# One head of the first searched place copied out by ScalarE in the sums of an attention and expert block

## The chip, the core and the metric

The kernel runs on one core of a Trainium2 chip. TensorE does matrix products into PSUM, VectorE does elementwise work and reductions, ScalarE does activations and copies, GpSimd (POOL) elementwise work and indirect DMAs, and SyncE (SP) issues most plain DMAs. The metric is the device time of one execution in microseconds (us). The time before is 2557.42 us, the median of three runs.

## What is computed

One transformer block on x of 4 x 2048 x 256, modulated by c: a layer norm, causal attention with 8 heads of width 32 and a geometric bias, a gated residual, a second layer norm, and an expert layer (2 shared experts, the best 4 of 16 routed ones for each token) with its gated residual. Cut to what matters here:

```python
scores = jnp.einsum('bhqd,bhkd->bhqk', q, k) * scale
scores = jnp.where(causal[None, None], scores, -jnp.inf)
scores = scores + head_scales[None, :, None, None] * geo
attn = jax.nn.softmax(scores, axis=-1)
out = jnp.einsum('bhqk,bhkd->bqhd', attn, v).reshape(B, T, C)
x = x + ga * (out @ w_out)
...
x = x + gb * ffn(h)          # 2 shared experts, top 4 of 16 routed
```

The softmax subtracts each row's maximum, so the kernel computes the scores twice: once to find the maximum (the search), and once, transposed, for the exponentials and the sums.

## The kernel before

**Tiles.** The 8192 tokens are 16 blocks `i` of 512 (QB); four blocks make one sequence, and `qb = i % 4` is the place in it. The 8 heads are two groups `g` of four. The scale and the geometric bias are folded into the key weights, so a score is a plain product.

**The search of block i** (`max_steps`, `scores(t, ch)` at line 425). For 128 queries `t` and a chunk `ch` of up to 512 keys (`w` of them), four products, one for each head, run at once in four strips of 32 rows of TensorE. Two heads go to one place (`both`, named ps) and two to the next. VectorE then finds each head's maximum in each place with one TENSOR_REDUCE over both heads, and writes it to `parts`. Where the chunk holds the diagonal (`ch == qb`), it first adds the causal mask to the last 128 columns of both heads, with `c_pair`, the mask repeated twice. `split` joins the parts, and `turn` brings the maxima into the layout that the sums need (`mT`).

**The sums of block i** (`sum_steps`, line 660 on). For each 128 keys `kb`, `probabilities` makes four transposed scores in two places (st): four products of 32 rows, four of 3 rows that subtract the maxima (the profile's st<-mT,unit), on the diagonal a mask product. Two exps on ScalarE write them to `pt` (p), one for each place. `weigh(kb, 0)` is the product with v (av) and `weigh(kb, 1)` the product with ones (dv). VectorE forms the reciprocal of dv at the end of each group (rd).

**PSUM.** `mring` (line 149) has three places of two banks, 128x2x512 f32; each of the two heads of a place has a bank. A place is taken in program order by the next user and is free when all that read it are done. A set of scores takes two places, an st takes two. `accp` has the other two banks, for av and dv during the sums.

**Order.** Every engine runs its instructions in the order in which the program issues them (`Pinned`). A block alternates between two phases. `fill_in` mixes projections, the expert work and searches of block i+1. Then come the sums of block i, with `state["summing"]` true; the searches of block i+1 that are left (`rest`) are placed among them. In the sums, step n issues: st of kb n; av of kb n-1; then, where there is one, a set of scores; dv of kb n-1; then small steps (norms, the choice of experts) and the `tick` that issues gathers and scatters. `paced` (line 496) makes each of these indirect DMAs wait for the last ScalarE instruction issued so far.

**Rings in SBUF.** `small` has three buffers for each tag, among them `log`, the router's logits, written by `logits` in `turn_steps` (line 846) between two sums and read by `choice_steps` in the sums that follow. `probs` has two buffers for each tag and is there once the setup is done.

Of the kernel before, what the change touches and what calls it, by code (L numbers as in the profile page):

```python
# [12 lines left out]
F32 = mybir.dt.float32  # L13
AF = mybir.ActivationFunctionType
ALU = mybir.AluOpType
AX = mybir.AxisListType
# [3 lines left out]
P = 128  # L20
QB = 512
TT = QB // P
# [70 lines left out]
def adaln_block_kernel(  # L93
# [13 lines left out]
    nc = Engines(tc)  # L107
# [5 lines left out]
    R = router.shape[2]  # L113
# [30 lines left out]
    small = ctx.enter_context(tc.tile_pool(name="small", bufs=3))  # L144
# [6 lines left out]
    state = {"single": 0, "summing": False, "pairs": True}  # L151

    def pair(name):

        return mring.tile([P, 2, QB], F32, tag="m", name=name)

    def single(shape, name):

        n = state["single"]
        state["single"] = (n + 1) % 5  # L160
        if not state["summing"] and (state["pairs"] or n % 5 in (0, 2)):
            return accp.tile(shape, F32, tag="acc", name=name)
        bank = pair(name)[:, 0, : math.prod(shape[1:])]
        dims = " ".join("abc"[: len(shape) - 1])
        sizes = dict(zip("abc", shape[1:-1]))
        return bank.rearrange(f"p ({dims}) -> p {dims}", **sizes)
# [37 lines left out]
    cmask = const.tile([P, P], F32, tag="cmask", name="cmask")  # L204
# [14 lines left out]
    c_pair = cmask.unsqueeze(1).broadcast_to([P, 2, P])  # L219
# [198 lines left out]
    def max_steps(i, g):  # L418

        qb = i % NB  # L420
        parts = small.tile([P, TT, 4, NB], F32, tag="parts", name=f"parts{i}_{g}")
        mTs[i, g] = work.tile([P, QB], BF16, tag=f"mT{g}", name=f"mT{i}_{g}")
        steps = []

        def scores(t, ch):
            w = min(QB, (qb * TT + t + 1) * P - ch * QB)
            halves = []
            for a in range(2):
                both = pair(f"ps{i}_{g}_{t}_{ch}_{a}")
                halves.append(both)  # L430
                for u in range(2):
                    r = G * (2 * a + u)
                    nc.tensor.matmul(
                        both[:, u, :w],
                        lhsT=qTs[i][r : r + G, g, t * P : (t + 1) * P],
                        rhs=kT[r : r + G, (i - qb + ch) % SLOTS, g, :w],
                        start=True,
                        stop=True,
                        tile_position=(r, 0),
                    )  # L440
            for a, both in enumerate(halves):
                if ch == qb:
                    edge = both[:, :, w - P : w]
                    nc.vector.tensor_tensor(edge, edge, c_pair, ALU.add)
                nc.vector.tensor_reduce(
                    parts[:, t, 2 * a : 2 * a + 2, ch], both[:, :, :w], AX.X, ALU.max
                )

        def split():
            pc = pieces[g]  # L450
            ngm = small.tile([P, TT, 4], F32, tag="ngm", name=f"ngm{i}_{g}")
            nc.vector.tensor_reduce(ngm, parts[:, :, :, : qb + 1], AX.X, ALU.max, negate=True)
            for n in range(3):
                nc.vector.tensor_copy(pc[:, :, :, n], ngm)
                if n < 2:
                    nc.vector.tensor_tensor(ngm, ngm, pc[:, :, :, n], ALU.subtract)

        def turn():
            pc = pieces[g]
            pr = single([P, QB], f"pr{i}_{g}")  # L460
            for t in range(TT):
                nc.tensor.matmul(
                    pr[:, t * P : (t + 1) * P],
                    lhsT=pc[:, t].rearrange("p h n -> p (h n)"),
                    rhs=ident_b,
                    start=True,
                    stop=True,
                )
            nc.scalar.copy(mTs[i, g], pr)

        for t in range(TT):
            for ch in range(qb + 1):
                steps.append(lambda t=t, ch=ch: scores(t, ch))
        return steps, split, turn
# [184 lines left out]
    probs = ctx.enter_context(tc.tile_pool(name="probs", bufs=2))  # L659
# [158 lines left out]
    logs = {}  # L818

    def turn_steps(i):  # L820

        h2 = h2s[i]

        def turn(ch):
            if ch == 0:
                tag = "hT" if i == NBLK - 1 else "h2T"
                h2Ts[i] = once.tile([P, KC, QB], F32, tag=tag, name=f"h2T{i}")
            pt = single([P, QB], f"ptb{i}_{ch}")
            for t in range(TT):
                nc.tensor.transpose(  # L830
                    pt[:, t * P : (t + 1) * P], h2[:, t, ch * P : (ch + 1) * P], ident
                )
            nc.scalar.copy(h2Ts[i][:, ch, :], pt)

        def logits():
            pl = single([P, TT, R], f"pl{i}")
            for t in range(TT):
                for k in range(KC):
                    nc.tensor.matmul(
                        pl[:, t, :],  # L840
                        lhsT=h2Ts[i][:, k, t * P : (t + 1) * P],
                        rhs=rw[:, k, :],
                        start=(k == 0),
                        stop=(k == KC - 1),
                    )
            logs[i] = small.tile([P, TT, R], F32, tag="log", name=f"log{i}")
            nc.scalar.copy(logs[i], pl)

        return [(T_US, lambda: turn(0)), (T_US, lambda: turn(1)), (2.2, logits)]
# [629 lines left out]
    i, j = DENSE  # L1479
# [62 lines left out]
```

## Time and profile before

| | |
|---|---|
| time, median of 3 runs | 2557.42 us (2553.51 to 2558.43) |
| the profiled execution's own time | 2559.8 us |
| its span, first to last instruction | 2558.1 us |
| mean granted clock of TensorE | 0.954 |
| searches (TENSOR_REDUCE into parts) | 640, 662.4 us of VectorE |
| exps of the sums (p<-st) | 640, 538.4 us of ScalarE |
| st products with q and k | 2560, 421.0 us |
| ps products | 2560, 387.8 us |
| chain that ended last, by engine | TensorE 75%, VectorE 12%, ScalarE 4%, issue 4% |

How to read the profile's lines: a group's line has source line, engine, operation, what it writes <- what it reads, shapes (partitions x elements), the count, then busy time in us and mean duration in ns, then idle time of the engine just before these instructions and what ended it. Nearly all lines of code are a helper's (L52), so groups are told apart by the names of their tiles. A line of the timeline has the start in us, the duration in us, engine, operation, names, shapes, count, and in brackets the idle time before it with what ended that. PE is TensorE, PEld its weight loads, DVE VectorE, ACT ScalarE. A float32 product appears as two MATMUL records with two loads, so one set of four heads has eight of each. A line of the stages' table has the stretch, its length, busy time (and count) of PE, PEld, DVE, ACT and POOL, the granted clock, the DMA share and GB/s.

### The profile page before, as it was taken

Reading aid. Unit: us, or ns where it says so; the run is one execution under the profiler, and the core shown is the slowest. Engines: PE = TensorE matmul, PEld = TensorE weight load, DVE = VectorE, ACT = ScalarE, POOL = GpSimd, SP = SyncE. Lnnn points to the kernel's source line nnn. Section 1 sums busy time; section 2 is a strip of 40 time slices with the busy share of each in tenths; the row PEclk is TensorE's granted clock in tenths of the full one; section 3 lists DMA queues with packets and bytes.
Section 4 is the critical chain, followed back from the end, with each engine's and each line's share of the span. In section 5 each row is a group of like instructions: output and inputs, shape, how many; then the busy total and the mean of one; then the engine's idle time right before and its main releaser. Section 6 shows DMA issues by size and latency. Waiting matters only on the chain.

```text
span 2558.1 us, 42345 instructions
## 1 busy us (share of the span) xinstructions
PE 2386.6 (93%) x16961; PEld 1165.1 (46%) x16961; DVE 1405.7 (55%) x2609; ACT 977.6 (38%) x1372; POOL 701.4 (27%) x740
## 2 busy tenths in 40 slices
PE   7999999999999899999999999999898999997987
PEld 4443424345554223355654335254545643345754
DVE  5576665526666855347565566346664564422235
ACT  2223233543433234544343344643344345542320
POOL 3201010411133144202015332401442025543234
PEclk9889899999999899999999999998999999998999
DMA  2300401434432112223742235233636843247943
GB/s 87 118 1 9 148 9 42 153 127 149 154 118 63 44 58 81 75 75 101 228 136 79 73 108 173 75 101 100 214 122 215 260 144 98 89 145 264 313 135 111
DMA packets 219701, 306.90 MB, mean 120 GB/s; under 512 B 18544, under 2 KB 158832, under 8 KB 219504
## 3 DMA queue, kind: packets, MB, share of 16 engines
q1 hardware_dynamic: 192720, 228.89, 27.4%
q0 software_dynamic: 25536, 73.43, 9.1%
q8 instruction: 134, 2.20, 0.4%
q10 hardware_dynamic: 1248, 1.86, 0.2%
q14 instruction: 63, 0.52, 0.1%
HBM read 193.49 MB, written 114.82 MB: 121 GB/s over the span
## 4 chain that ended last, share of the span: by engine, by line
PE 75%; DVE 12%; ACT 4%; issue 4%; POOL 2%; DMA 2%; SPq 0%; POOLq 0%; ACTq 0%; DVEq 0%
PE st L52 15%; PE ps L52 12%; PE av L52 9%; PE dv L52 8%; PE pu L52 7%; PE py L52 5%; DVE parts L52 4%; PE po L52 3%; PE ppq L52 2%; PE pv L52 2%; PE px L52 2%; PE ppk L52 2%; DVE rd L52 2%; PE pd_s L52 1%; PE pd L52 1%
## 5 line engine op out<-in xcount | busy, mean ns | idle before, releaser
L52 DVE TENSOR_REDUCE parts<-ps 128x2 f32<-128x1024 f32 (+3 forms) x640 | 662.4, 1062 | 348.6 <-PE ps L52 339.6
L52 ACT ACTIVATE p<-st 128x1024 f32<-128x1024 f32 (+3 forms) x640 | 538.4, 893 | 652.8 <-PE st L52 652.5
L52 PE MATMUL st<-qT,kv 32*128 32x512 f32 (+3 forms) x2560 | 421.0, 594 | 32.8 <-DVE parts L52 21.0
L52 PE MATMUL ps<-kv,qT 32*128 32x512 f32 (+3 forms) x2560 | 387.8, 608 | 16.9 <-DVE parts L52 9.7
L52 POOL DMA_INDIRECT got<-yg,at x224 | 219.5, 980 | 399.7 <-ACT p L52 134.1
L52 PE MATMUL av<-p,kv 128*32 128x512 f32 (+3 forms) x2560 | 312.5, 561 | 4.6 <-DVE rd L52 4.6
L52 PE MATMUL dv<-p,ones 128*32 128x512 f32 (+3 forms) x2560 | 303.3, 546 | 0.0
L72 POOL DMA_INDIRECT xg<-rows,at x219 | 213.2, 974 | 266.9 <-ACT p L52 109.7
L52 PEld LDWEIGHTS st<-qT,kv 32*128 32x128 f32 x2560 | 141.0, 189 | 295.8 <-issue 209.2
L52 DVE TENSOR_TENSOR ps<-ps,cmask 128x256 f32<-128x256 f32 x256 | 109.3, 427 | 266.3 <-PE ps L52 245.9
L52 PEld LDWEIGHTS ps<-kv,qT 32*128 32x128 f32 x2560 | 127.8, 192 | 207.1 <-issue 112.9
L52 POOL TENSOR_TENSOR x<-x,tmps 128x512 f32<-128x512 f32 x28 | 35.4, 1263 | 623.1 <-DVE tmps L52 623.0
L52 PE MATMUL py<-wt,tact 128*128 128x256 f32 x608 | 163.8, 403 | 7.7 <-ACT xt L52 3.5
L52 PEld LDWEIGHTS pu<-xt,wt 128*128 128x128 f32 x1216 | 150.5, 197 | 29.5 <-issue 11.5
L52 PE MATMUL pu<-xt,wt 128*128 128x128 f32 x1216 | 158.3, 284 | 4.8 <-DMA wt<-experts 3.7
L52 PE MATMUL st<-mT,unit 3*128 3x512 bf16 (+3 forms) x1280 | 162.3, 353 | 0.0
L52 PEld LDWEIGHTS dv<-p,ones 128*32 128x32 f32 x2560 | 74.0, 111 | 173.9 <-issue 167.0
L52 DVE SCALAR_TENSOR_TENSOR sum<-got,weight,sum 128x256 f32<-128x256 f32 x168 | 82.9, 494 | 123.3 <-DMA got<-yg,at 119.5
L52 ACT COPY y<-py 128x512 f32<-128x512 f32 x152 | 89.0, 586 | 155.0 <-PE py L52 154.4
L52 PEld LDWEIGHTS py<-wt,tact 128*128 128x128 f32 x608 | 109.8, 195 | 57.6 <-issue 15.2
L52 ACT COPY xt<-px 128x512 f32<-128x512 f32 x152 | 86.9, 586 | 101.1 <-PE px L52 100.5
L52 PEld LDWEIGHTS av<-p,kv 128*32 128x32 f32 x2560 | 53.8, 109 | 140.1 <-issue 118.7
(287 smaller groups left out, 2425.9 us busy)
## 6 DMA issues: line engine op xcount, KB each, us to landing
wt<-experts SPq DMA_DIRECT2D x304, 256.0 KB, 4.3
xr<-xg SPq DMA_DIRECT2D x76, 512.0 KB, 4.6
yg<-y SPq DMA_DIRECT2D x76, 512.0 KB, 3.5
xg<-zeros SPq DMA_DIRECT2D x16, 1024.0 KB, 10.0
xin<-in_x SPq DMA_DIRECT2D x16, 512.0 KB, 6.2
x<-in_x SPq DMA_DIRECT2D x16, 512.0 KB, 4.5
h2d<-xnb POOLq DMA_DIRECT2D x14, 512.0 KB
pre<-x POOLq DMA_DIRECT2D x14, 512.0 KB, 3.4
```

What stands on the lines that cost most here:

```text
L52: made = call(*args, **kwargs)
L72: made = call()
```

## The change

In the sums only, `scores` lets ScalarE copy the second head of the first place into a new SBUF tile (`second`, 128x512 f32, two buffers). VectorE searches the first head, then the second place with both of its heads as before, and then the copy. On the diagonal, the mask is added for one head in the place, for two heads in the second place, and for the copied head in SBUF. Outside the sums, nothing is different. The ring of the logits has two buffers in place of three.

```diff
-            for a, both in enumerate(halves):
+            def top(scores, h0, h1, mask):
                 if ch == qb:
-                    edge = both[:, :, w - P : w]
-                    nc.vector.tensor_tensor(edge, edge, c_pair, ALU.add)
-                nc.vector.tensor_reduce(
-                    parts[:, t, 2 * a : 2 * a + 2, ch], both[:, :, :w], AX.X, ALU.max
-                )
+                    edge = scores[..., w - P : w]
+                    nc.vector.tensor_tensor(edge, edge, mask, ALU.add)
+                nc.vector.tensor_reduce(parts[:, t, h0:h1, ch], scores[..., :w], AX.X, ALU.max)
+
+            if state["summing"]:
+
+                copy = probs.tile([P, QB], F32, bufs=2, tag="second", name=f"second{i}_{g}_{t}_{ch}")
+                nc.scalar.copy(copy[:, :w], halves[0][:, 1, :w])
+                top(halves[0][:, 0, :], 0, 1, cmask)
+                top(halves[1], 2, 4, c_pair)
+                top(copy, 1, 2, cmask)
+            else:
+                top(halves[0], 0, 2, c_pair)
+                top(halves[1], 2, 4, c_pair)
...
-            logs[i] = small.tile([P, TT, R], F32, tag="log", name=f"log{i}")
+            logs[i] = small.tile([P, TT, R], F32, bufs=2, tag="log", name=f"log{i}")
```

## The prediction

> **What bounds the kernel now.** I read the page's busy times first, then the groups kept apart by shape, then the waits, then the timeline of the sums.
>
> ```profile
> PE 2386.6 (93%) x16961; PEld 1165.1 (46%) x16961; DVE 1405.7 (55%) x2609; ACT 977.6 (38%) x1372; POOL 701.4 (27%) x740
> ...
> L52 DVE TENSOR_REDUCE parts<-ps 128x2 f32<-128x1024 f32 x448 | 529.9, 1221 | 342.0 <-PE ps L52 339.6
> L52 DVE TENSOR_TENSOR ps<-ps,cmask 128x256 f32<-128x256 f32 x256 | 109.3, 427 | 266.3 <-PE ps L52 245.9 <-ACT p L52 19.4 <-ACT y L52 0.7
> L52 DVE TENSOR_REDUCE parts<-ps 128x2 f32<-128x512 f32 x64 | 44.3, 693 | 2.2
> L52 ACT COPY num<-av 128x512 f32<-128x512 f32 x32 | 18.9, 589 | 10.3 <-PE av L52 10.3
> ```
>
> TensorE is busy 93%, so VectorE and ScalarE have room on average, and the page's waits of TensorE for VectorE's searches are small (st 21.0 us, ps 9.7 us). That understates them. A set of scores runs four heads at once; when two heads are held, the other two run, and TensorE counts as busy. The timeline shows it. First a slot in which the search was done early, then a masked slot and an unmasked one in which it was not:
>
> ```profile
> 933.41 2.36 DVE L52 TENSOR_REDUCE parts<-ps 128x2 f32<-128x1024 f32 x2 [5.19 <-PE ps L52]
> 934.85 0.31 PEld L52 LDWEIGHTS st<-qT,kv 32*128 32x128 f32 x8 [1.35 <-issue]
> 934.86 1.14 PE L52 MATMUL st<-qT,kv 32*128 32x512 f32 x8
> 939.43 1.29 PE L52 MATMUL st<-qT,kv 32*128 32x512 f32 x8
> ```
> ```profile
> 947.61 0.43 DVE L52 TENSOR_TENSOR ps<-ps,cmask 128x256 f32<-128x256 f32 x1 [2.21 <-PE ps L52]
> 948.08 0.96 DVE L52 TENSOR_REDUCE parts<-ps 128x2 f32<-128x768 f32 x1
> 948.49 0.30 PEld L52 LDWEIGHTS st<-qT,kv 32*128 32x128 f32 x4 [0.84 <-issue]
> 949.15 0.22 PEld L52 LDWEIGHTS st<-qT,kv 32*128 32x128 f32 x2 [0.37 <-issue]
> ...
> 953.55 0.65 PEld L52 LDWEIGHTS st<-qT,kv 32*128 32x128 f32 x8 [0.84 <-issue]
> 953.56 1.48 PE L52 MATMUL st<-qT,kv 32*128 32x512 f32 x8
> 955.16 1.94 ACT L52 ACTIVATE p<-st 128x1024 f32<-128x1024 f32 x2 [2.80 <-PE st L52]
> 956.18 1.19 PE L52 MATMUL ps<-kv,qT 32*128 32x512 f32 x8
> 957.36 2.36 DVE L52 TENSOR_REDUCE parts<-ps 128x2 f32<-128x1024 f32 x2 [2.37 <-PE ps L52]
> 957.38 0.97 POOL L72 DMA_INDIRECT xg<-rows,at  x1 [3.77 <-ACT p L52]
> ```
>
> Undisturbed, eight loads go in 0.31 us. In the masked slot the last four come 0.66 us after the first (948.49 to 949.15), just behind the first place's search (end 949.04). The slot from 953.56 to 958.29 takes 4.73 us, the one from 934.86 to 939.43 takes 4.57. The ring has three places: a set of scores takes two, the next st takes the third and the one that this search frees first. So the first search sets the second half of the next st.
>
> **What the change frees.** It touches scores computed inside the sums. The loops give 101 of the 320 there: 61 unmasked and 40 masked. The first place held until both of its heads were searched; it is now held until VectorE has one and ScalarE has copied the other.
>
> The search of one 512 costs what one of 2x256 costs, 693 ns; two heads cost 1221. So VectorE lets go 0.53 us earlier. ScalarE's copy takes 589 ns (num, also 128x512 out of PSUM). It stands behind the two exps, which end at 957.10; the scores end at about 957.36, so the copy ends near 957.95 and the search near 958.05: VectorE still decides, by 0.1 us. For a masked 512 the release was 0.43+0.03+1.22 = 1.68 us after the start. One head's mask of 128 isn't in the trace; it lies between 0.17 (16-element rows) and 0.43 (256). On the line through 64 elements (rpr, 0.22) and 256 it is 0.29. That gives 0.29+0.69 = 0.98: 0.70 us earlier (0.56 to 0.82 over the bounds). Likewise 384 wide 0.57, 256 wide 0.43.
>
> I went through all 101 in the timeline and took how late the second half of the next st starts, less the usual 0.05 us, where the search had just ended. The total is 54 us. Each gets back the smaller of its lateness and the earlier release; 0.03 us of the lateness is free, because the first exp then holds the next ps (937.14 in the first slot takes 1.36 us, not 1.19). 4.73 - 4.57 = 0.16 for 0.19 us of lateness gives that 0.03.
> - 36 unmasked, late by less than 0.6 us, 7.9 us in all: 6.8 back.
> - 14 unmasked, later (VectorE was at a reciprocal of 3.35 us or a norm), 22.3 us: 14 x 0.53 = 7.4 back.
> - 13 masked 512: 8.5; 8 of 384: 3.3; 7 of 256: 2.7. The remaining 23 were not late: 0.
>
> Sum 28.7 us; with the mask's bounds 26 to 30.
>
> **What it adds.** VectorE: three searches for two, 2x0.693+1.221-2x0.08 (records overlap by 0.08) = 2.44 against 2.36, and for a masked 512 3.54 against 3.28. 61x0.08+40x0.26 = 15 us. It comes behind the release, so it costs only where TensorE waits for other VectorE results: pk 9.7, pr 9.3, pc 7.4, av 4.6 us, 21 waits. 21x0.17 = 3.6; I take 3, bounds 0 and 15.
>
> [...]
>
> ScalarE: 101 copies, at most 0.59 us each, 60 us. They are hidden in ScalarE's idle time of 2.6 to 2.8 us before each pair of exps; the copy takes it from about 957.36 to 957.95, and the next exp comes 1.6 us after 958.29. Uncovered it would cost 60 us. Behind the waiting copy stand the next exps, num, mT and rpr copies; the exps need a later st anyway. The two copy buffers wait for a search two slots earlier, 9 us, while the longest lateness of a search is 4.3: nothing.
>
> TensorE: the second half of st now waits for two engines, which takes a separate wait instruction (51 ns where masked slots have one). Bounds 0 and 101x0.05 = 5; I take 2.
>
> POOL: each gather or scatter waits for ScalarE's last instruction, now the copy: 957.95 for 957.10, 0.85 us later. 85 of these DMAs lie in the three stretches 738 to 799, 846 to 972 and 1413 to 1526 us: at most 72 us. I take 0: POOL had been idle 3.77 us, and there VectorE waited for a gather once (0.57 us at 786).
>
> The logits' ring of 3 becomes 2: written between sums, read in the next, one alive at a time. Nothing; without that cover, one ScalarE wait for VectorE per block. No DMA is added or moved.
>
> Sum against the profiled execution: 2558.1 - 28.7 + 3 + 2 = 2534.4 us of span. The run with that span took 2559.8; the runs shown have a median of 2557.4, so 2557.4 - 23.7 = 2533.7, say 2533.
>
> **The clock** can add to it:
>
> ```profile
> 371.00:378.00 7.00, 5.01 (x40) 1.43 (x36) 5.64 (x6) 1.88 (x3) 0.00 (x0) 1.00 0.01 2
> 927.70:934.50 6.80, 6.80 (x30) 1.14 (x26) 1.61 (x2) 1.94 (x2) 0.97 (x1) 0.50 0.07 22
> ```
>
> After the stalls that end at 135, 780, 927 and 1482 us (2.7 to 4.1 us) the granted clock is 0.50 for 20.4 us in all, 10 us lost; after the stall of 3.0 us that ends at 376 it stays 1.00. Shorter by 0.4 to 0.5 us, some may no longer halve it. I put 0 in the sum and up to 10 us in the range's low end.
>
> [...]
>
> **Rivals.**
> - *The time goes to the exps.* The first exp holds the next ps in every slot, and the short latenesses come back in full. Left: 7.4+14.5 masked, less 5: 2557.4-17 = 2540. For it: the ps of 1.36 us. Against: the slot with it was still the shorter one.
> - *It doesn't do what it says.* If mask and copy of one place shut each other out, the masked search starts 0.6 us later and gains 0.1 instead of 0.7; unmasked gains stay: 28.7-14.5+2-5 = 11, giving 2546. Against: they read different heads. If the unmasked ones are serialized as well, nothing is left: 2557 plus or minus 3.
> - *ScalarE becomes the bound*, the one that ends slower: the copy waits for the scores with the exps behind it, and av waits for the exps. It decides where more than 1.9 us of delay sit ahead of the copy (ScalarE's slack to the next exp). Uncovered, 60 us - 28.7 + 5 = +36, 2594; break-even is 24/0.59 = 40 uncovered copies. Against: in all 101 slots the copy would have ended before the old release.
>
> **How the numbers follow.** As worked 0.58, exps 0.14, shut out 0.12 (of it 0.06 with nothing left), ScalarE 0.09, POOL's pacing or new half-clock phases above the gain 0.07. A measurement here can tell some 0.2%, 5 us, from no change. Faster: 0.58+0.14+0.06 and 0.01 of the last = 0.79; same: 0.06 and 0.02 of the last; slower: 0.09 and 0.04 of the last = 0.13. The likeliest gives 2533, its own range 2516 (clock, higher bounds) to 2545. To leave out no more than 2 in 10, the range reaches 2514 to 2556.
>
> **What would show it.** Right: loads of st behind unmasked scores in some 0.35 us instead of 0.65; slots of 4.57 us for 4.73; copies of 0.59 us directly behind pairs of exps; masked latenesses at 0.1 to 0.2; VectorE up 15 us and ScalarE up 55. Wrong: TensorE waiting more for p, copies that start over a microsecond after the scores, VectorE idle before a head's search on the copy, or a lower mean clock than 0.954.

## The result, and the profile after

The changed kernel takes 2579.23 us (median of 6, 2573.34 to 2590.27), beside 2557.53 us for the kernel before in the same job (6 executions): a ratio of 1.0087 [1.0063, 1.0111], some 22 us slower. A second time it gave 1.0081 [1.0064, 1.0099]. The profiled execution took 2579.4 us with a span of 2577.7 us and a mean granted clock of 0.951 (before 0.954).

The page's busy times, and the new instructions as the view of the tile `second` gives them (minimum/median/maximum ns, then the shapes):

```profile
PE 2401.5 (93%) x16961; PEld 1160.6 (45%) x16961; DVE 1416.7 (55%) x2750; ACT 1030.3 (40%) x1473; POOL 702.6 (27%) x740
```
```profile
L52 ACT COPY second<-ps x101: 265/585/594, 108.9 to 1954.9; 128x512 f32<-128x512 f32 x76, 128x384 f32<-128x384 f32 x12, 128x256 f32<-128x256 f32 x7, 128x128 f32<-128x128 f32 x6
L52 DVE TENSOR_REDUCE parts<-second x101: 286/676/687, 111.3 to 1958.4; 128x1 f32<-128x512 f32 x76, 128x1 f32<-128x384 f32 x12, 128x1 f32<-128x256 f32 x7, 128x1 f32<-128x128 f32 x6
L52 DVE TENSOR_TENSOR second<-second,cmask x40: 280/281/340, 117.7 to 1958.1; 128x128 f32<-128x128 f32 x40
```

The count of 101 and the prices are those forecast: 585 ns for 589, 281 ns for a mask that was put at 0.29 us. VectorE is up 11.0 us and ScalarE 52.7. So the added work has the size foreseen; what it costs lies elsewhere, and the waits show where (engine and tile that wait, what ended it: us in all, times, longest):

```profile
DVE ps L52 <- ACT second L52: 175.1, 36, 17.8
DVE parts L52 <- ACT second L52: 123.1, 49, 7.1
PEld st L52 <- ACT second L52: 65.1, 80, 1.5
PEld ps L52 <- DVE parts L52: 58.6, 72, 1.9
```

The first two are new: in 85 of the 101 slots VectorE's first mask or search of a place is released last by ScalarE's copy out of that place. Their 298 us are not a loss of 298 us (VectorE waited for the scores before; only the last bit is the copy), but they say that the two engines don't read the place at the same time. The last two are mostly no new waiting: undisturbed loads of st also come 0.84 us after the loads ahead of them, and while the third line has 65.1 us, the loads of st that the profile puts down to "issue" fall from 209.2 to 154.1 us. The timeline of an unmasked and a masked slot shows what that does:

```profile
961.95 1.18 PE L52 MATMUL ps<-kv,qT 32*128 32x512 f32 x8
...
963.17 0.59 ACT L52 COPY second<-ps 128x512 f32<-128x512 f32 x1 [0.30 <-ACT p L52]
963.79 1.82 DVE L52 TENSOR_REDUCE parts<-ps 128x1 f32<-128x512 f32 x2 [2.44 <-ACT second L52]
964.06 0.30 PEld L52 LDWEIGHTS st<-qT,kv 32*128 32x128 f32 x4 [0.84 <-ACT second L52]
...
964.53 0.19 PEld L52 LDWEIGHTS st<-qT,kv 32*128 32x128 f32 x2 [0.17 <-DVE parts L52]
...
967.81 0.48 ACT L52 COPY second<-ps 128x384 f32<-128x384 f32 x1
968.33 0.30 DVE L52 TENSOR_TENSOR ps<-ps,cmask 128x128 f32<-128x128 f32 x1 [2.12 <-ACT second L52]
...
968.66 0.56 DVE L52 TENSOR_REDUCE parts<-ps 128x1 f32<-128x384 f32 x1
968.70 0.30 PEld L52 LDWEIGHTS st<-qT,kv 32*128 32x128 f32 x4 [0.84 <-ACT second L52]
...
969.33 0.22 PEld L52 LDWEIGHTS st<-qT,kv 32*128 32x128 f32 x2 [0.33 <-issue]
```

Copy from 963.17 to 963.76, and only then the search of head 0, from 963.79 to 964.48 (the 1.82 us are two searches). From the scores' end at 963.13 that is 1.35 us, against 1.22 before: the place comes free 0.13 us later, not 0.53 earlier, and the second half of the next st waits for it (964.53). In the masked slot copy, mask and search follow one another and end at 969.22, 0.52 us behind the first st load; before, mask and search of both heads ended 0.55 us behind it (949.04 after 948.49). Nothing is gained there.

For all 101 slots I sum how late the fifth weight load of the next st comes behind the fourth, less the usual 0.05 us, and call it the lateness: 64.6 us before (64.1 in a second profile), 72.3 after (71.2). This takes in every cause of a late second half; the prediction's 54 us counted only those where the search had just ended.

The rest of the loss lies in the clock. I take the sums as the time from each block's first st load to its last, added over the 16 blocks, and split off what the stretches at half clock (granted clock 0.50) lose, put at half of their length (in the profile before a 512-wide st product with q and k takes 1056 ns in them, median, for 588 at 1.00):

| us | sums, without what half clock loses | lost to half clock in the sums |
|---|---|---|
| before, its second profile | 1145.4, 1143.1 | 52.1, 53.7 |
| after, its second profile | 1155.1, 1152.0 | 65.5, 65.8 |

So the sums grow by some 22 us, of which 9 to 10 are waits (the lateness is 7 to 8 of them) and 12 to 13 are half clock. Over the timed executions of the second job (`after_again`) the granted clock gives a smaller share: (1 - clock) x span is 117.8 us on average before (11 executions) and 122.8 after (6; 124.2 in the first job), 5 to 6 us more. Two stretches of block 3 after the change (columns as in the table of stages; PEclk is third from the end) show such a pair:

```profile
465.80:469.10 3.30, 1.50 (x17) 0.52 (x13) 2.68 (x14) 0.11 (x1) 0.00 (x0) 1.00 1.09 386
469.16:472.50 3.34, 3.34 (x20) 0.57 (x16) 3.24 (x6) 1.94 (x2) 0.00 (x0) 0.50 0.41 144
```

TensorE is busy 1.50 of 3.30 us and the next 3.34 us, in which it is busy throughout, run at 0.50. Block 3 lost nothing to half clock before and 3.4 us after.

### The profile page after: what moved, and what is told of

Same layout as the page of the kernel before. It is cut to its first block, busy times and chain, and to the rows that moved or that the text cites. A ratio compares the mean times of both kernels' runs of the same rounds, so it can differ in the third digit from the quotient of the medians.

```text
span 2577.7 us, 42596 instructions
## 1 busy us (share of the span) xinstructions
PE 2401.5 (93%) x16961; PEld 1160.6 (45%) x16961; DVE 1416.7 (55%) x2750; ACT 1030.3 (40%) x1473; POOL 702.6 (27%) x740
## 4 chain that ended last, share of the span: by engine, by line
PE 75%; DVE 11%; ACT 4%; issue 4%; POOL 3%; DMA 3%; SPq 0%; POOLq 0%; ACTq 0%; DVEq 0%
PE st L52 15%; PE ps L52 12%; PE av L52 10%; PE dv L52 8%; PE pu L52 6%; PE py L52 5%; DVE parts L52 4%; PE po L52 2%; PE ppq L52 2%; PE pv L52 2%; PE px L52 2%; PE ppk L52 2%; PE pd L52 1%; PE pd_s L52 1%; DMA wt<-experts 1%
## 5 line engine op out<-in xcount | busy, mean ns | idle before, releaser
L52 DVE TENSOR_REDUCE parts<-ps 128x2 f32<-128x1024 f32 (+6 forms) x640 | 614.4, 987 | 361.8 <-PE ps L52 229.7
L52 PE MATMUL st<-qT,kv 32*128 32x512 f32 (+3 forms) x2560 | 428.5, 596 | 33.5 <-DVE parts L52 21.8
L72 POOL DMA_INDIRECT xg<-rows,at x219 | 213.5, 975 | 275.5 <-ACT second L52 64.5
L52 PEld LDWEIGHTS st<-qT,kv 32*128 32x128 f32 x2560 | 140.8, 189 | 306.2 <-issue 154.1
L52 DVE TENSOR_TENSOR ps<-ps,cmask 128x256 f32<-128x256 f32 (+1 forms) x256 | 104.0, 406 | 276.8 <-ACT second L52 175.1
```

The source lines that it names most:

```text
L52: made = call(*args, **kwargs)
L72: made = call()
```

## The experiments

Four theories. (1) Taking turns: the program orders ScalarE's copy and VectorE's first search of one place, so each delays the other and the place is held longer. (2) VectorE's added work: three searches for two, and an extra mask. (3) Half clock: shifted stalls halve the clock more often. (4) ScalarE's load: 60 us of copies ahead of the exps and the gathers that are paced by ScalarE.

The chips differ: the kernel before has a median of 2555.7 to 2557.5 us in the jobs of `after`, `after_again`, `before_again`, `e6_idle_copy` and `e7_both_bf16`, of 2582.1 in that of `e1` to `e4`, of 2579.1 in that of `e5`, `e8`, `e9` and the first `e10`, and of 2589.9 in the last. Ratios are always to the kernel before on the same chip, and an expectation in us is to be read beside a kernel before of some 2557 us. Lateness is compared between jobs as well: it is 64.6, 64.1 and 64.1 us in three profiles of three jobs that search as the kernel before does (the third is e5's).

**The order taken away (e1_free).** The changed kernel, with the dependency between the copy and the first search (and mask) of the same place dropped. They read different heads. In `top`, `made` holds the mask and the search.

```diff
-                nc.scalar.copy(copy[:, :w], halves[0][:, 1, :w])
-                top(halves[0][:, 0, :], 0, 1, cmask)
+                made = nc.scalar.copy(copy[:, :w], halves[0][:, 1, :w])
+                apart = f"apart{i}_{g}_{t}_{ch}"
+                tc.add_to_no_dep_group(apart, made.ins)
+                top(halves[0][:, 0, :], 0, 1, cmask, apart)
...
+                if apart is not None:
+                    for one in made:
+                        tc.declare_no_dep(one.ins, group=apart, reason="another bank")
```

> The change, with the order between ScalarE's copy of head 1 and VectorE's mask and search of head 0 taken away (they read different banks of the place); each still waits for its own products, and the place is free when both are done. Theory 1 (the two readers of one place take turns, so the first search starts only when the copy ends): the search starts with the copy, the first place comes free 0.5 to 0.7 us earlier than in the changed kernel, st's second half starts with its first half in unmasked slots, and the time falls to 2530 to 2545 us. Theory 2 (VectorE's extra searches and masks cost the time): stays at 2570 to 2580. Theory 3 (only phases of the half clock differ): 2557 to 2580, following the mean granted clock, with slots of the same length as in the changed kernel at full clock.

Measured: 2563.86 us, ratio 0.993 [0.9903, 0.9957]. The timeline of an unmasked slot:

```profile
935.68 0.31 PEld L52 LDWEIGHTS st<-qT,kv 32*128 32x128 f32 x8 [0.84 <-ACT second L52]
...
937.97 1.36 PE L52 MATMUL ps<-kv,qT 32*128 32x512 f32 x8
...
939.12 1.82 DVE L52 TENSOR_REDUCE parts<-ps 128x1 f32<-128x512 f32 x2 [2.16 <-PE ps L52]
939.17 0.59 ACT L52 COPY second<-ps 128x512 f32<-128x512 f32 x1
...
940.25 0.31 PEld L52 LDWEIGHTS st<-qT,kv 32*128 32x128 f32 x8 [0.84 <-ACT second L52]
940.25 1.14 PE L52 MATMUL st<-qT,kv 32*128 32x512 f32 x8
```

Search and copy start 0.05 us apart, all eight loads of st go in 0.31 us, and the slot, from one st to the next (935.68 to 940.25), takes the forecast's 4.57 us. On the first chip the ratio would be 2540 us, in the range that theory 1 gave. The lateness falls to 33.5 us, 39 below the changed kernel's; the ratios of the two kernels are 1.6% apart, some 40 us. Taking turns is the cause, and the fall in lateness has the size of its price. Side by side the copy takes 0.59 us and the two searches 1.82 us, as in the changed kernel, where the searches follow the copy; the order there is the program's, not the memory's.

**The search split, no copy (e2_split).** VectorE searches the two heads of the first place one after the other; ScalarE does nothing new.

```diff
-                nc.scalar.copy(copy[:, :w], halves[0][:, 1, :w])
                 top(halves[0][:, 0, :], 0, 1, cmask)
+                top(halves[0][:, 1, :], 1, 2, cmask)
                 top(halves[1], 2, 4, c_pair)
-                top(copy, 1, 2, cmask)
```

> No copy: VectorE searches head 0, head 1 and then the second place, all from PSUM, so only the split of one search (and mask) in two is left of the change, and the shorter logits' ring. Theory 1: the first place comes free 0.1 us later than before (0.69+0.61 for 1.22 us; masked 0.3 later), so 2560 to 2567 us, well under the changed kernel. Theory 2: 2572 to 2582, like the changed kernel.

Measured: 2593.47 us, 1.0049 [1.0028, 1.007], lateness 75.5 us. By the prediction's prices the split holds the place 0.08 us longer (0.26 masked); it lets VectorE do the added work, and it costs half a per cent, 11 us, between the ranges of the two theories. But the lateness is up by 11 us as well, so nothing is left that the work behind the release would have to explain: theory 2 isn't shown here, and e1 carries about the same work of VectorE and gains.

**The search first, then the copy (e3_search_first).** The two lines are exchanged.

> The copy is issued behind the search of head 0, so now ScalarE waits for VectorE and no search waits for a copy. Theory 1 (taking turns): the first place is held for search plus copy, 0.69+0.59 and some 0.05 us between, as in the changed kernel (1.3 for 1.22 us before), but the second place is searched 0.6 us earlier; 2565 to 2578. Where VectorE comes late, ScalarE's copy comes late with it, with the next exps behind it: no better than the changed kernel there. Theory 2: 2572 to 2582.

Measured: 2594.61 us, 1.0046 [1.0029, 1.0063]. The waits show the turn taken the other way round:

```profile
ACT second L52 <- DVE parts L52: 156.4, 93, 6.6
```

Now ScalarE stands behind VectorE, 93 times and up to 6.6 us, with the exps queued behind the waiting copy. The lateness of st is 61.6 us, no more than before, but half clock takes 73.7 us of the sums. So the kernel loses with the other engine first too, though not through the lateness; what brings the half clock isn't shown.

**Both heads copied (e4_both1).** ScalarE copies both heads of the first place (one f32 buffer), and VectorE searches the second place and then the copy with both heads. No place has two readers.

```diff
-                nc.scalar.copy(copy[:, :w], halves[0][:, 1, :w])
-                top(halves[0][:, 0, :], 0, 1, cmask)
+                nc.scalar.copy(copy[:, :, :w], halves[0][:, :, :w])
                 top(halves[1], 2, 4, c_pair)
-                top(copy, 1, 2, cmask)
+                top(copy, 0, 2, c_pair)
```

> ScalarE copies both heads of the first place (128x1024, some 1.02 us by the exps' rows) into one buffer, VectorE searches the second place first and then the copy, so no place has two readers. Theory 1: the first place is free 1.02 us after the scores where nothing holds ScalarE, whatever VectorE is at: the latenesses of 54 us in all fall under 15, 2515 to 2535 us. Against it: the single buffer ties the next copy to VectorE's search of the last one; if that or ScalarE's added 100 us decide (theory 4), 2560 to 2590 with TensorE waiting for p.

Measured: 2548.92 us, 0.9883 [0.9859, 0.9906], lateness 10.6 us. ScalarE copies twice as much as in the change and the kernel gains 1.2%: theory 4 can't be the main one.

**The kernel again, and the one before again.** 

> The changed kernel as it is, beside the kernel before on the chip of this job. All theories: a ratio of 1.005 to 1.012, as on the other chip. If it stands at the ratio of the split alone and of the copy behind the search (1.005), the loss is nearly the same in all three; theory 1 has it at or above these two.

> The kernel before, for its profile on the chip of this job. The stretches outside the sums should differ from the first profile by the same 7 to 11 us as those of the experiments did, and the sums little; that would make the higher times of the kernel before a matter of the chip.

The changed kernel: 2579.32 us, 1.0081 [1.0064, 1.0099]. The kernel before: 2553.91 us in one execution, lateness 64.1 us. The loss and its traces repeat. This chip is no slower than the first, so what the second expectation says of the chips isn't tested by it.

**A copy that nobody reads (e6_idle_copy).** The copy is made as in the change, and VectorE searches both heads in the place as before, behind it. The copy is not used, so VectorE has no added work.

```diff
                 nc.scalar.copy(copy[:, :w], halves[0][:, 1, :w])
-                top(halves[0][:, 0, :], 0, 1, cmask)
+                top(halves[0], 0, 2, c_pair)
                 top(halves[1], 2, 4, c_pair)
-                top(copy, 1, 2, cmask)
```

> The copy is made and nobody reads it; VectorE searches both heads of both places in PSUM with one instruction each, as before. So no search is split and VectorE has no added work; only ScalarE's copy and its turn at the first place are added. Theory 1: the first search starts 0.6 us later, behind the copy, and the first place is held 1.85 for 1.22 us; st's second halves come late by 45 to 60 us more in all, ratio 1.012 to 1.028, worse than the changed kernel. Theory 2 (VectorE's added work): 0.998 to 1.002.

Measured: 2613.04 us, 1.0209 [1.0188, 1.0231], lateness 105.5 us. A slot of it:

```profile
974.86 0.59 ACT L52 COPY second<-ps 128x512 f32<-128x512 f32 x1 [0.31 <-PE ps L52]
975.48 2.36 DVE L52 TENSOR_REDUCE parts<-ps 128x2 f32<-128x1024 f32 x2 [3.04 <-ACT second L52]
...
975.74 0.30 PEld L52 LDWEIGHTS st<-qT,kv 32*128 32x128 f32 x4 [0.84 <-ACT second L52]
...
976.76 0.19 PEld L52 LDWEIGHTS st<-qT,kv 32*128 32x128 f32 x2 [0.72 <-DVE parts L52]
...
981.14 0.30 PEld L52 LDWEIGHTS st<-qT,kv 32*128 32x128 f32 x4 [0.84 <-ACT second L52]
```

The search starts 0.03 us after the copy's end, the second half of st comes 1.02 us behind the first, and the slot takes 5.40 us (975.74 to 981.14). With no work added to VectorE, the turn costs 2.1%, some 53 us, more than the change, which gives part of it back by the shorter search. The lateness is 41 us of that; the load on ScalarE, which this run has as well, is taken by itself in e8.

**Both heads as bfloat16 (e7_both_bf16).** As e4, with the copy in bfloat16 (the maxima of these heads are rounded to it) and two buffers.

```diff
-                copy = probs.tile([P, QB], F32, bufs=2, tag="second", name=f"second{i}_{g}_{t}_{ch}")
+                copy = probs.tile(
+                    [P, 2, QB], BF16, bufs=2, tag="second", name=f"second{i}_{g}_{t}_{ch}"
+                )
```

> Both heads copied by ScalarE as in the fourth experiment, but as bfloat16 and into two buffers. The maxima that the softmax subtracts are rounded to bfloat16 for these heads (the same value is subtracted above and below the division). If the single buffer tied ScalarE to VectorE in the slots where VectorE is late, the ratio falls from 0.988 to 0.980 to 0.986; if it cost nothing, 0.986 to 0.990.

Measured: 2514.28 us, 0.9823 [0.9804, 0.9842], lateness 9.5 us. A slot in which VectorE is busy elsewhere shows one source of the gain:

```profile
902.30 3.35 DVE L52 RECIPROCAL rd<-rd 128x512 f32<-128x512 f32 x1
...
903.04 0.59 ACT L52 CAST second<-ps 128x512 bf16<-128x512 f32 x1
...
903.92 0.31 PEld L52 LDWEIGHTS st<-qT,kv 32*128 32x128 f32 x8 [0.84 <-ACT second L52]
```

VectorE sits in a reciprocal until 905.65; the place is free at 903.63 all the same, and eight loads go in 0.31 us. In the kernel before five slots with such a reciprocal held half of st up by 2.6 to 4.1 us.

**ScalarE's load alone (e8_load_only).** ScalarE makes 101 copies of the same width out of SBUF (keys), which nobody reads; VectorE searches as before.

```diff
-                nc.scalar.copy(copy[:, :w], halves[0][:, 1, :w])
-                top(halves[0][:, 0, :], 0, 1, cmask)
+                nc.scalar.copy(copy[:, :w], kT[:, (i - qb + ch) % SLOTS, g, :w])
+                top(halves[0], 0, 2, c_pair)
```

> ScalarE makes 101 copies of the same size in the same places, but of keys in SBUF, and nobody reads them; VectorE searches as before. No place is shared, so only ScalarE's load and the later start of the DMAs paced by its last instruction are added. Theory 1: the load is hidden in ScalarE's idle time before the next exps: 0.998 to 1.003. Theory 4 (ScalarE's time or the pacing costs): 1.004 to 1.020, 60 us of copies being the most.

Measured: 2589.02 us, 1.0025 [1.0002, 1.0048], lateness 63.4 us. The copies that were held to be hidden cost some 6 us of 60 (0.5 to 12 by the interval), and in the profile beside that of e5 the sums are 5.8 us shorter without half clock and lose 6.8 us more to it. These copies never wait for scores, with the exps queued behind them, as those of the change do, so that part of ScalarE's load isn't in this number.

**The logits' ring alone (e5_log).** The kernel before with `bufs=2` for `log`.

> The kernel before with two buffers for the logits in place of three, nothing else. All theories: no difference, 0.998 to 1.002.

Measured: 2579.68 us, 0.9998 [0.9976, 1.002]. Nothing, as forecast.

**One bfloat16 buffer (e9_bf16_one).** e7 with `bufs=1`, and later e7 and this one on one chip.

> Both heads copied as bfloat16 into one buffer in place of two. If the second buffer made the difference between 0.988 and 0.982: 0.985 to 0.990. If not (bfloat16, or a difference between the chips of the two jobs): 0.980 to 0.985.

> Both heads copied as bfloat16 (the maxima are rounded to it), two buffers: 0.982 again. If the second buffer makes the gain over one buffer (0.9876 on another chip), this is 0.4 to 0.7% under the one-buffer kernel beside it; if the chips made the difference, the two are equal to 0.2%.

> The same with one buffer: 0.987 to 0.989 if the second buffer matters, 0.982 to 0.984 if the chip made the difference.

Measured: 0.9876 [0.9843, 0.9908] at first, which looked as if the second buffer were worth half a per cent. Side by side they are equal: e7 2548.56 us, 0.9851 [0.9814, 0.9888]; e9 2548.95 us, 0.9859 [0.982, 0.9898]. The buffer is worth nothing that can be told, and that reading fell.

**Only the masked scores (e10_masked_only).** The change for the 40 masked scores alone.

```diff
-            if state["summing"]:
+            if state["summing"] and ch == qb:
```

> The change for the 40 masked scores alone; the 61 unmasked ones are searched as before. Theory 1: there the turn (copy 0.59, mask 0.30, search 0.69) gives the first place back after 1.65 us for 1.68 before, neither gain nor loss: 0.999 to 1.004, so that the loss of the whole change lies in the unmasked scores, where the turn makes 1.32 us of 1.22. Theory 2 (VectorE's added work, two thirds of which is in the masked scores): 1.005 to 1.008.

Measured: 2595.75 us, 1.0053 [1.0029, 1.0078]. Theory 1's numbers missed, and theory 2's range (1.005 to 1.008) was met: I had held that masked places, free no later than before, cost nothing. The lateness is 63.3 us indeed. Beside e5, on the same chip, the sums are 4.5 us shorter without half clock and lose 14.4 us more to it, as stalls that are no longer but lie elsewhere would; that was not tried by itself.

**The masked scores, with and without the order.** e10 again, and e10 with the dependency dropped as in e1 (e11_masked_free).

> The change for the 40 masked scores alone with the order kept, again, on the chip of the one with the order taken away: 1.0053 [1.0029, 1.0078] if that was no chance of its chip; 0.999 to 1.003 if it was.

> The change for the 40 masked scores alone, with the order between copy and first search taken away. Taking turns (theory 1): these are released some 0.5 us earlier and half of them follow a late slot, 14 us back by the prediction's sum: 0.993 to 0.998 of before, and at least 0.5% under the masked scores with the order kept (1.0053 so far). Added work of VectorE (0.26 us for each of 40 scores, theory 2): the order is not what costs here, and this stays within 0.3% of the masked scores with the order kept, 1.002 to 1.008.

Measured, on one chip: with the order 2603.83 us, 1.0053 [1.003, 1.0076]; without it 2587.41 us, 0.9997 [0.9979, 1.0014]. The order costs 0.56% here too, so theory 1 holds where e10 had put it in doubt; but the gain over the kernel before that it foresaw did not come. Lateness 64.5 against 51.4 us: 13 of the 14.5 us that the prediction's sum gives for these scores are won, and given back elsewhere. Between the two profiles the sums differ by 17.3 us, 10.2 without half clock and 7.1 in it. What gives the 13 us back was not tried by itself: the added masks and searches of VectorE (40 x 0.26 = 10 us), ScalarE's copies and half clock are candidates, and no run parts them.

## Why the prediction was wrong

It said 2533 us and faster; 2579 is slower, and outside its range of 2514 to 2556.

**The step that failed** is the release of the first place: "the copy ends near 957.95 and the search near 958.05". It let both readers start with the scores' end; in the change VectorE's search starts when the copy is over (963.79 after 963.76), and the place is free 1.35 us after the scores where 0.69 was forecast and 1.22 was usual. The same assumption was weighed once, under the rival, and dropped with "they read different heads". That argues from the data; the wait is set by the program, and the program orders the two engines by the place, whose two banks are one tile. Nothing in the profile of before could show it, as no place there had readers on two engines, and that was the reason to give the rival more than 0.06 for its full form. Had the terms been added with the turns taken (0.59 + 0.03 + 0.69 = 1.31 us for 1.22, and 1.65 for 1.68 masked), the 28.7 us would have been gone, and a loss of some 10 us left: 61 x 0.09 for the longer turns and the 5 us charged for added work.

**The rival that named the mechanism** was wrong in its size as well. It left "2557 plus or minus 3", and the kernel takes 22 us more. What it lacked: the place held 0.1 us longer (lateness up 7 to 8 us), and 5 us (over the executions of a job) to 13 us (in the profiled sums) of half clock.

**What held.** With the order gone, the arithmetic of the slots is right to the hundredth: 4.57 us, x8 loads in 0.31. The forecast of -23.7 us (0.991) lies in e1's interval (0.9903 to 0.9957), but at its edge and by terms that partly cancel: against the kernel before the lateness falls by 31 us for 28.7 forecast, while the time falls by some 18, so that about 13 us are lost elsewhere where the sum charged 5. Copy, mask and the counts of 61 and 40 slots were right, and the logits' ring was nothing (e5).

**Terms mis-sized.** ScalarE's copies were put at 0 and cost about 6 us (e8). VectorE's added work was put at 3 us, since it lies behind the release, and no run shows more: the split alone (e2) loses 11 us, and its lateness grows by 11. An estimate points the same way. If a microsecond of lateness is a microsecond of time, what is left is 8 to 24 us in each of the kernels with copies by ScalarE, the change (14) and the idle copy (12) among them, and 2 us in e2, which has none, each uncertain by some 5 us. That points to the copies for the rest of the loss; by what way they bring it isn't shown. The separate wait instruction of TensorE, put at 2 us, did not come: the profile has 346 semaphore waits in TensorE's queue before and 349 after, since the search, always last, releases the place alone; with the order gone (e1) there are 409. The clock was put at 0 with a gain of up to 10 us in the range, and went the other way: in the profiled sums the copies of one head, the split and even the idle load lose 61 to 74 us to half clock, the kernels before (with e5) 52 to 56, and only the copies of both heads stay at 52 to 60. The sign of that term was open, and the range had it on one side only. POOL's pacing, put at 0, shows waits of gathers and scatters for the copy (xg and got, 68.6 and 40.4 us), but VectorE's waits for gathered rows do not rise (125.7 us for 128.8 before).

**Still open:** why half clock takes more in nearly all kernels with moved stalls, by what way ScalarE's copies cost time beside the lateness, and what takes the 13 us back in e11.

## What to carry to other kernels

Two engines that read different banks of one tile may still be taking turns: before splitting a reader between engines, look for whether the program orders them, and either take that order away (0.993 here) or give each tile a single reader. Freeing the tile whole through the engine that has time (both heads by ScalarE: 0.988 with float32, 0.982 to 0.988 with bfloat16) beat both kernels and every half measure. When parts of a set of products run beside each other, TensorE's busy share of 93% hides half-sets that wait; sum how late the second half starts instead.

## What the hardware showed

**Half clock lies on a grid.** In the profiles of before and after all changes between full and half clock lie, to 0.002 us, on one grid of 3.413 us, whose phase differs between the two (2.64 and 1.49 us from the span's start); 33 of 34 and 35 of 36 stretches at half clock are 1 to 4 steps long (3.4, 6.8, 10.2, 13.7 us), and the profile before has some 69 such steps, after 74, with 1.7 us put down as lost in each. The same stall is followed by half clock in one run and not in another: after the half of st that is 2.92 us late in block 2, at 372 to 376 us, both profiles of the kernel before keep 1.00, and e5's loses 3.4 us. So a change that moves stalls can't be costed by their lengths alone.

**Chips differ by 1%, and the profile shows a part of it.** The kernel with the smaller logits' ring takes 22 us more on its chip than the kernel before on the first, while both are alike on one chip. Of its sums 13 us are neither half clock nor lateness. One place, TensorE in block 15 (no scores there), first on the slower chip, then the same products before on the first:

```profile
2251.13 0.64 PE L52 MATMUL av<-p,kv 128*32 128x256 f32 x4 [0.63 <-issue]
2252.55 0.38 PE L52 MATMUL av<-p,kv 128*32 128x256 f32 x1 [0.78 <-issue]
...
2253.98 0.65 PE L52 MATMUL dv<-p,ones 128*32 128x256 f32 x5 [0.78 <-issue]
```
```profile
2232.80 0.61 PE L52 MATMUL dv<-p,ones 128*32 128x256 f32 x8
```

There TensorE issues a few products at a time with gaps of 0.6 to 0.8 us for which the profile shows no wait, and the slot takes 5.55 us for 1.82. It is no chance of one run: the waits of TensorE have 7 to 14 gaps put down to "issue", 4.6 to 10.2 us, in each of the 12 profiles from the slower chips, and none in the six from the faster ones. That is at most half of the difference; what holds the issue up isn't shown, nor where the rest lies.
